# Attention scores of the first layer over three bfloat16 pieces in place of float32, with the exponentials one unit further behind

## The chip, the cores and the metric

The kernel runs on one core of a Trainium2 chip. The metric is the device time of the program in microseconds; the median of several runs counts. A core has five engines that run beside each other, each with its own queue of instructions in a fixed order: TensorE (PE in the profile, with its weight loads shown apart as PEld), VectorE (DVE), ScalarE (ACT), GpSimd (POOL) and SyncE (SP), which here only issues DMA transfers. They wait for each other by semaphores.

## The reference, cut to what matters

The program is a chain of residual blocks on a tensor of 4 batches x 512 tokens x 128 features, all float32:

```
x = x + 0.5 * latent_ffn(layernorm(x))   # causal attention, 16 heads of 8, then 8 experts, 2 chosen per token
x = x + attention(layernorm(x))          # full attention, 16 heads of 8
x = x + 0.5 * latent_ffn(layernorm(x))   # as the first
x = x + 0.5 * chosen_ffn(layernorm(x))   # attention of chosen tokens
x = x + additive_attention(layernorm(x)) # four layers
x = x + 0.5 * chosen_ffn(layernorm(x))
```

The change lies in the first three lines, which the kernel calls the first layer. What it computes there for every head (q and k have 8 values a token):

```
scores = q @ k.T / sqrt(8)          # causal: only keys up to the query
a      = exp(scores - max(scores)) / sum(exp(scores - max(scores)))
out    = a @ v
```

## The kernel before, in words

**Tasks and units.** The first layer is twelve tasks: four causal ones ("latent", one a batch), four full ones, four causal ones. A task's 16 heads lie as four groups g of four heads j. In the tiles `qA` and `kA` head j takes partitions 32j to 32j+31, so that a matmul of one head uses 32 of the array's 128 rows, and four heads can be multiplied at once on four strips of rows. A unit is one bank width of scores (512 columns) for all four heads of a group: 16 units in a full task. A causal task has 10, since the triangle is left out; four of them hold one piece of 512 columns, four hold 384 + 128, two hold 256 + 256.

**Two passes over the scores.** For each unit the queries are first multiplied with the keys (`maxima`, line 527) and VectorE takes the maximum of every row into `nms` (`reduce_max`: line 543 adds the causal mask and takes the maximum in one instruction, line 547 is the plain maximum of the full tasks). When a group is complete, `place_maxima` transposes its maxima (line 551) and four DMAs (line 555) write them into row 1 of each strip of `qA`; `kA` holds -1 in that row. Some units later `shifted` (line 562) multiplies again with keys and queries swapped, and this time the product comes out less the maximum. ScalarE takes its exponential (`exponent`, line 574), GpSimd zeroes the upper triangle of causal blocks (`mask`, line 580), and `products` (line 605) multiplies with the values.

**The order.** `attention` is one loop over units n. Every unit has two halves. In each half two heads of unit n go through `maxima` and two heads of an earlier unit through `shifted`, so four strips are busy; then come the maxima on VectorE, the exponentials, the mask, half of a unit's `products` two units later (`LAG`), and one piece of other work. `behind[n]` says which unit `shifted` takes: five units behind in the beginning (`FIRST`), one more from unit 26 (`HOLD`), at which `shifted` takes none. `GAP` is that distance; the next task but one may overwrite `qA` and `kA` (two sets, in turn) when it has passed.

**Other work beside it.** `prepare` makes a task's normalised input, queries `qC` and keys `kC` (lines 346 and 351, one ScalarE copy each out of PSUM). `spread` copies them by DMA to the strips of `qA` and `kA` (lines 359 and 360 for the first task, 363 to 366 for the others). `Mixture` computes the experts of a finished causal task (`hidden`: lines 467, 472, 473; `combined`), one step a half.

**What a scheduler decides.** The program is recorded by a layer that puts each engine's instructions in an order by its own estimate of when they are ready. That order is then fixed: an instruction that waits holds up all behind it on its engine. PSUM banks are chosen by `bank` with a small clock of its own.

Of the kernel before, what the change touches and what calls it, by code (L numbers as in the profile page):

```python
# [8 lines left out]
F32 = mybir.dt.float32  # L9
BF16 = mybir.dt.bfloat16  # L10
AF = mybir.ActivationFunctionType
ALU = mybir.AluOpType
AX = mybir.AxisListType

P = 128
B = 4
NC = 4
T = NC * P
NG = 4
NH = 16  # L20
HD = P // NH
FIRST, HOLD = 5, [26]
GAP, LAG = 6, 2
NE = 8
FH = 2
KSEL = T // 8
# [14 lines left out]
def tile_macaron(ctx: ExitStack, tc: tile.TileContext, a: dict, out: bass.AP):  # L41
    nc = tc.nc

    const = ctx.enter_context(tc.tile_pool(name="const", bufs=1))
# [6 lines left out]
    free, clock = [0.0] * 8, [0.0]  # L51
# [42 lines left out]
    causal = const.tile([P, T], F32, name="causal")  # L94
    paired = const.tile([P, P], BF16, name="paired")
    ones = const.tile([P, T], F32, name="ones")
    zeros = const.tile([4, T], F32, name="zeros")
    before = const.tile([P, NE, NE], F32, name="before")
    slots = const.tile([P, KSEL], F32, name="slots")
    places = const.tile([P, T], F32, name="places")  # L100
# [131 lines left out]
    def first_layer(opened, picked):  # L232
        with (
# [3 lines left out]
        ):  # L237
            hp = streaming.enter_context(tc.tile_pool(name="heads", bufs=1))

            qAs = [hp.tile([P, NG, T], F32, name=f"qA{i}") for i in range(2)]  # L240
            kAs = [hp.tile([P, NG, T], F32, name=f"kA{i}") for i in range(2)]
            vAs = [hp.tile([P, NC, NH, 32], F32, name=f"vA{i}") for i in range(2)]


            nc.vector.memset(qAs[0], 0.0)
            nc.vector.memset(kAs[0], -1.0)

            nms = [hp.tile([P, 32], F32, name=f"nm{g}") for g in range(NG)]
            for nm in nms:
                nc.gpsimd.memset(nm[:, 16:32], 0.0)  # L250

            def heads_constants():
                constants()
# [22 lines left out]
            class Task:  # L276
# [24 lines left out]
                def prepare(self):  # L301

                    b = self.b
# [7 lines left out]
                    v = small.tile([P, 2 * NC], F32, name="v2")  # L311
# [30 lines left out]
                    self.src = src  # L342
                    ps = bank()
                    by_columns(ps, wq, hT)
                    self.qC = wp.tile([P, T], F32, name="qC", bufs=1)
                    nc.scalar.activation(self.qC, ps, AF.Copy, scale=HD**-0.5)
                    yield
                    ps = bank()
                    by_columns(ps, wk, src)
                    self.kC = wp.tile([P, T], F32, name="kC", bufs=1)  # L350
                    nc.scalar.copy(self.kC, ps)
                    self.ready = True

                def spread(self):


                    if self.k == 0:
                        for g in range(NG):
                            nc.sync.dma_start(self.qA[0:P:4, g, :], self.qC[g:P:4, :])
                            nc.scalar.dma_start(self.kA[0:P:4, g, :], self.kC[g:P:4, :])  # L360
                        return
                    if self.k > 1:
                        nc.sync.dma_start(self.qA[1:P:32], zeros[0:4, :].unsqueeze(1).to_broadcast([4, NG, T]))

                    nc.sync.dma_start(self.qA[0:P:4], self.qC)
                    nc.sync.dma_start(self.kA[0:P:4], self.kC)

                def values(self):
                    pv = bank()
# [140 lines left out]
            def attention():  # L510
# [7 lines left out]
                def first(t, c, w):  # L518

                    return T - w, NC - 1 - c if t.causal else c  # L520

                def maxima(n, j):
                    t, unit = units[n]
                    ps = bank((2.0 if len(unit) == 1 else 2.3) + (0.8 if len(unit) == 1 else 1.1) * (j % 2))
                    r0 = 32 * j
                    for g, c, at, w in unit:
                        nc.tensor.matmul(  # L527
                            ps[:, at : at + w],
                            lhsT=t.qA[r0 : r0 + 32, g, c * P : (c + 1) * P],
                            rhs=t.kA[r0 : r0 + 32, g, 0:w],  # L530
                            start=True,
                            stop=True,
                        )
                    return ps

                def reduce_max(n, j, ps):
                    t, unit = units[n]
# [9 lines left out]
                            nc.vector.tensor_reduce(dst, src, axis=AX.X, op=ALU.max)  # L547

                def place_maxima(t, g):
                    mT = wp.tile([P, 32], F32, name="mT")  # L550
                    nc.vector.transpose(mT, nms[g])

                    to = t.qA[1:P:32, g, :].rearrange("j (c u q) -> j c u q", c=NC, u=4)
                    for u in range(4):
                        nc.sync.dma_start(to[:, :, u, :], mT[32 * u : 32 * u + 16, :])

                def shifted(n, j, ps):
                    t, unit = units[n]
                    r0 = 32 * j
                    for g, c, at, w in unit:  # L560
                        q0, kc = first(t, c, w)
                        nc.tensor.matmul(  # L562
                            ps[:, at : at + w],
                            lhsT=t.kA[r0 : r0 + 32, g, kc * P : (kc + 1) * P],
                            rhs=t.qA[r0 : r0 + 32, g, q0:T],
                            start=True,
                            stop=True,
                        )
                    return ps

                def exponent(n, j, ps):
                    if n not in es:
# [50 lines left out]

                behind = [None] * FIRST + list(range(HOLD[0] - FIRST))
                for h0, h1 in zip(HOLD, HOLD[1:] + [len(units) + GAP]):
                    x0 = behind[-1] + 1
                    behind += [None] + list(range(x0, x0 + h1 - h0 - 1))
                for n in range(len(units) + GAP + LAG):
                    now[0] = n
# [10 lines left out]
                    for part in range(2):  # L640
                        halves[0] += 1
                        sj, xj = (0, 1) if part == 0 else (2, 3), (2, 3) if part == 0 else (0, 1)
                        if n < FIRST:
                            sj = () if part else (0, 1, 2, 3)
                        xp, sp = [], []
                        if s is not None and n < 2 * FIRST:
                            sp = [maxima(s, j) for j in sj]
                        if x is not None:
                            xp = [shifted(x, j, bank(1.9 + 0.5 * i)) for i, j in enumerate(xj)]
                        if s is not None and n >= 2 * FIRST:  # L650
                            sp = [maxima(s, j) for j in sj]
                        clock[0] += 1.1
                        for j, ps in zip(sj, sp):
                            reduce_max(s, j, ps)
                        for j, ps in zip(xj, xp):
                            exponent(x, j, ps)
                        if x is not None and units[x][0].causal:
                            mask(x, xj[0])
                        one_hidden()
                        if y is not None:  # L660
                            products(y, part)
                        one_combined()
                        if part == 0:
                            for f in todo:
                                f()
                        step_background()
# [89 lines left out]
            nc.scalar.copy(f_wkv, ps[:, 0 : 2 * P])  # L756
            for _ in tasks[0].prepare():
                pass
            nc.vector.memset(qAs[1], 0.0)
            nc.vector.memset(kAs[1], -1.0)  # L760
            with tc.issue_after(last_root[0]):
                heads_constants()
            tasks[0].spread()
# [612 lines left out]
```

## Time and profile before

| what | value |
|---|---|
| median of 3 runs | 1371.02 us (1368.14 to 1375.04) |
| profiled execution: span from the first to the last instruction | 1369.7 us |
| profiled execution: time of its own outside the span | not recorded; the median is 1.3 us over the span |
| PE busy | 1289.1 us, 94% |
| DVE busy | 954.4 us, 70% |
| ACT busy | 586.5 us, 43% |
| POOL busy | 562.1 us, 41% |
| first `maxima` matmul starts | 17.36 us |
| last `maxima` of the twelfth task | 772.6 us |
| `maxima` matmuls of line 527 | 1536, 349.0 us busy |
| `shifted` matmuls of line 562 | 1536, 334.0 us busy |

How to read it: the page has two PE records for each float32 matmul of the program, so the 1536 of line 527 are 768 matmuls. Busy times of one engine overlap where matmuls run side by side. By the start of every 128th record of line 527 the tasks begin at 17.4, 57.1, 100.7, 167.2, 239.0, 347.6, 435.3, 496.1, 556.9, 599.8, 642.5 and 707.4 us. The experts' steps (line 473) run from 131.9 to 399.5 us and from 681.0 to 883.6 us. Everything after about 884 us is outside the change.

### The profile page before, as it was taken

The page shows a single profiled execution, that of the slowest core. Times are in us where ns is not written, and L with a number is a line of the kernel's source. Part 1 is how long each engine was busy: PE and PEld are TensorE (multiplying, and loading weights), DVE is VectorE, ACT ScalarE, POOL GpSimd, SP SyncE. Part 2 cuts the span into 40 slices and gives each one's busy share as a digit, 9 for nine tenths or more (in the row PEclk, how much of TensorE's full clock was granted, in tenths as well). Part 3 has the DMA queues.
Part 4 walks back from the last instruction along what each step waited for, and adds up shares of the span by engine and source line. Part 5 has one row for each costly group of instructions (what it writes and reads, how often), then busy time and mean ns, then how long its engine had stood idle before and what let it go on. Part 6 is the DMA issues. An engine that isn't in the chain of part 4 may idle for free. (4 is left out here: it accounts for less than half of the span.)

```text
span 1369.7 us, 29349 instructions
## 1 busy us (share of the span) xinstructions
PE 1289.1 (94%) x11050; PEld 699.9 (51%) x11050; DVE 954.4 (70%) x3293; ACT 586.5 (43%) x1180; POOL 562.1 (41%) x823
## 2 busy tenths in 40 slices
PE   5998999999999999999999999989889999997897
PEld 2554445333333333465544443367667767665675
DVE  6886776666658777778767638687466776667773
ACT  1555454454556666665545443222223332323222
POOL 8345655544424112024564755622244443543100
PEclk8999999999999999999999999999979999999799
DMA  3001101020111100000111011211000100000000
GB/s 115 21 24 41 43 33 49 2 80 1 64 45 32 39 1 18 3 19 19 50 33 34 33 53 28 76 40 40 1 20 5 40 1 17 1 1 1 1 9 23
DMA packets 37172, 39.52 MB, mean 29 GB/s; under 512 B 11080, under 2 KB 23880, under 8 KB 37032
## 3 DMA queue, kind: packets, MB, share of 16 engines
q1 hardware_dynamic: 34536, 35.06, 8.3%
q10 hardware_dynamic: 2496, 2.59, 0.6%
q8 instruction: 87, 1.43, 0.4%
q14 instruction: 53, 0.43, 0.1%
HBM read 29.45 MB, written 1.18 MB: 22 GB/s over the span
## 5 line engine op out<-in xcount | busy, mean ns | idle before, releaser
L574 ACT ACTIVATE e<-bank 128x512 f32<-128x512 f32 x576 | 313.7, 595 | 278.4 <-PE bank L527 240.0
L527 PE MATMUL bank<-kA,qA 32*128 32x512 f32 (+3 forms) x1536 | 349.0, 527 | 4.1 <-DVE nm L543 1.8
L562 PE MATMUL bank<-qA,kA 32*128 32x512 f32 (+3 forms) x1536 | 334.0, 524 | 0.3 <-DVE nm L543 0.3
L543 DVE CUSTOM_DVE_ANT_0 junk<-bank,causal 128x384 f32<-128x384 f32 (+3 forms) x512 | 251.0, 490 | 89.5 <-PE bank L527 51.3
L547 DVE TENSOR_REDUCE nm<-bank 128x1 f32<-128x512 f32 x256 | 164.9, 686 | 78.9 <-PE bank L527 78.7
L473 POOL TENSOR_TENSOR hid<-v,spread 128x512 f32<-128x512 f32 x128 | 163.9, 1286 | 127.1 <-DVE v L472 101.7
L562 PEld LDWEIGHTS bank<-qA,kA 32*128 32x128 f32 x1536 | 129.5, 185 | 136.9 <-issue 54.1
L605 PE MATMUL sum<-e,vA 128*32 128x256 f32 (+1 forms) x2560 | 183.7, 368 | 6.1 <-POOL e L580 6.0
L580 POOL TENSOR_SCALAR_AFFINE_SELECT e<-e 128x256 f32<-128x256 f32 x256 | 99.3, 407 | 192.8 <-ACT e L574 191.7
L527 PEld LDWEIGHTS bank<-kA,qA 32*128 32x128 f32 x1536 | 147.4, 187 | 24.6 <-DVE nm L543 5.8
L605 PEld LDWEIGHTS sum<-e,vA 128*32 128x32 f32 x2560 | 62.8, 109 | 165.8 <-issue 134.0
L267 PE MATMUL sum<-hid,sb_f_w 128*32 128x512 f32 x1024 | 135.6, 597 | 3.0 <-POOL hid L473 2.9
L267 PE MATMUL bank<-tT,sb_f_w 128*32 128x512 f32 x1024 | 137.1, 602 | 0.0
L472 DVE SCALAR_TENSOR_TENSOR v<-th,bank 128x512 f32<-128x512 f32 x128 | 87.0, 681 | 43.9 <-ACT th L467 29.2
L467 ACT ACTIVATE th<-bank 128x512 f32<-128x512 f32 x128 | 76.3, 597 | 49.0 <-PE bank L267 39.5
L154 POOL TENSOR_TENSOR r<-v,mhalf 128x4 f32<-128x4 f32 (+1 forms) x64 | 71.8, 1123 | 5.1
L1250 PE MATMUL bank<-h2T,w 128*128 128x512 f32 x128 | 69.0, 632 | 0.2 <-ACT h2T L1239 0.2
L1256 PE MATMUL bank<-w,hid 128*128 128x128 f32 x512 | 65.7, 277 | 0.1
L1256 PEld LDWEIGHTS bank<-w,hid 128*128 128x128 f32 x512 | 63.1, 194 | 4.8 <-issue 1.5
L1251 ACT ACTIVATE hid<-bank,sb_l_cols 128x512 f32<-128x512 f32 x64 | 43.9, 688 | 39.9 <-PE bank L1250 39.8
L1148 PE MATMUL bank<-wa,hT 128*128 128x385 f32 x128 | 56.5, 540 | 1.4 <-ACT hT L1141 1.4
L312 POOL TENSOR_SCALAR v<-mv 128x4 f32<-128x4 f32 x12 | 2.8, 230 | 131.1 <-DVE mv L171 130.8
(279 smaller groups left out, 1805.4 us busy)
## 6 DMA issues: line engine op xcount, KB each, us to landing
spread<-away SPq DMA_DIRECT2D x64, 256.0 KB
qA<-mT SPq DMA_DIRECT2D x192, 2.0 KB
qA<-qC SPq DMA_DIRECT2D x11, 256.0 KB
kA<-kC SPq DMA_DIRECT2D x11, 256.0 KB
w<-in_l_w_dram SPq DMA_DIRECT2D x8, 256.0 KB
sb_m_wqkv<-in_m_wqkv_dram SPq DMA_DIRECT2D x4, 384.0 KB
m_yg<-in_m_trig_dram SPq DMA_DIRECT2D x8, 130.0 KB
X<-in_x_dram SPq DMA_DIRECT2D x4, 256.0 KB
```

Source lines behind the costliest of these rows:

```text
L267: nc.tensor.matmul(ps[32 * j : 32 * j + 32, :], lhsT=w[:, 32 * j : 32 * j + 32], rhs=rhs, start=start, stop=stop, skip_group_check=True,)
L467: nc.scalar.activation(th, ph, AF.Tanh, scale=0.5)
L472: nc.vector.scalar_tensor_tensor(v, th, 1.0, ph, ALU.add, ALU.mult)
L473: nc.gpsimd.tensor_tensor(hid, v, self.spread[e], op=ALU.mult)
L527: nc.tensor.matmul(ps[:, at : at + w], lhsT=t.qA[r0 : r0 + 32, g, c * P : (c + 1) * P], rhs=t.kA[r0 : r0 + 32, g, 0:w], start=True, stop=True,
L543: nc.vector.tensor_tensor_reduce(junk[:, 0:w], src, causal[:, T - w : T], 1.0, NEG, ALU.add, ALU.max, dst)
L547: nc.vector.tensor_reduce(dst, src, axis=AX.X, op=ALU.max)
L562: nc.tensor.matmul(ps[:, at : at + w], lhsT=t.kA[r0 : r0 + 32, g, kc * P : (kc + 1) * P], rhs=t.qA[r0 : r0 + 32, g, q0:T], start=True, sto ...
L574: nc.scalar.activation(es[n][:, j, :], ps, AF.Exp)
L580: nc.gpsimd.affine_select(out=e, in_=e, pattern=[[0, 2], [1, P]], compare_op=ALU.is_ge, fill=0.0, base=0, channel_multiplier=-1,)
L605: nc.tensor.matmul(to[32 * j : 32 * j + 32, q0 + lo - at : q0 + hi - at], lhsT=t.vA[:, kc, 4 * j + g, :], rhs=es[n][:, j, lo:hi], start=fresh,
L1256: nc.tensor.matmul(pm[:, c * P : (c + 1) * P], lhsT=hid[:, f, c * P : (c + 1) * P], rhs=w2[:, f, :], start=(f == 0), stop=(f == 3),)
```

## The change

Queries, keys and maxima are each written as a sum of three bfloat16 numbers. The three pieces of a key lie in rows 0, 1, 2 of every four rows of the strip; three tiles `qA[0]`, `qA[1]`, `qA[2]` hold the three pieces of the queries, turned by one place from tile to tile, so that three bfloat16 matmuls that add up in one bank give all nine products. The negated row now takes four rows (3, 11, 19, 27) of a strip, three of which hold the pieces of the maximum.

In a half, the four strips now go round by round: first all matmuls with `qA[0]`, then all with `qA[1]`, then all with `qA[2]`. `pieces` replaces the single copy out of PSUM: ScalarE writes the first piece, VectorE the rest, GpSimd the second piece and the third. `place_maxima` splits the maxima by four GpSimd instructions ahead of the transposition, which becomes 128 columns wide. `spread` issues twelve DMAs of 128 KB where it issued two of 256 KB (eight of 64 KB for the first task). `behind` stands still at two units, 26 and 27, and `GAP` is 7.

```diff
-FIRST, HOLD = 5, [26]
-GAP, LAG = 6, 2
+FIRST, HOLD = 5, [26, 27]
+GAP, LAG = 7, 2
+NS = 3
...
-            qAs = [hp.tile([P, NG, T], F32, name=f"qA{i}") for i in range(2)]
-            kAs = [hp.tile([P, NG, T], F32, name=f"kA{i}") for i in range(2)]
+            qAs = [[hp.tile([P, NG, T], BF16, name=f"qA{i}{r}") for r in range(NS)] for i in range(2)]
+            kAs = [hp.tile([P, NG, T], BF16, name=f"kA{i}") for i in range(2)]
...
-            nc.vector.memset(qAs[0], 0.0)
-            nc.vector.memset(kAs[0], -1.0)
+            def fill(i):
+                for q in qAs[i]:
+                    nc.vector.memset(q.rearrange("p g t -> p (g t)").bitcast(F32), 0.0)
+                nc.vector.memset(kAs[i], -1.0)
+            fill(0)
...
-                    nc.scalar.activation(self.qC, ps, AF.Copy, scale=HD**-0.5)
+                    self.qC = self.pieces(ps, HD**-0.5, "q")
...
-                    nc.scalar.copy(self.kC, ps)
+                    self.kC = self.pieces(ps, 1.0, "k")
...
+                def pieces(self, ps, scale, name):
+                    x = [wp.tile([P, T], BF16, name=f"{name}C{s}", bufs=1) for s in range(NS)]
+                    rest = wp.tile([P, T], F32, tag="v", name="rest")
+                    nc.scalar.activation(x[0], ps, AF.Copy, scale=scale)
+                    nc.vector.scalar_tensor_tensor(rest, ps, scale, x[0], ALU.mult, ALU.subtract)
+                    nc.gpsimd.tensor_copy(x[1], rest)
+                    nc.gpsimd.tensor_tensor(x[2], rest, x[1], op=ALU.subtract)
+                    return x
...
-                    nc.sync.dma_start(self.qA[0:P:4], self.qC)
-                    nc.sync.dma_start(self.kA[0:P:4], self.kC)
+                    moves = [(self.kA[s:P:4], self.kC[s]) for s in range(NS)]
+                    moves += [(self.qA[r][s:P:4], self.qC[(s + r) % NS]) for r in range(NS) for s in range(NS)]
+                    for i, (to, x) in enumerate(moves):
+                        (nc.scalar if self.k == 0 and i % 2 else nc.sync).dma_start(to, x)
...
-                    for g, c, at, w in unit:
-                        nc.tensor.matmul(ps[:, at : at + w], lhsT=t.qA[r0 : r0 + 32, g, c * P : (c + 1) * P],
-                            rhs=t.kA[r0 : r0 + 32, g, 0:w], start=True, stop=True)
-                    return ps
+                    def product(r):
+                        for k, (g, c, at, w) in enumerate(unit):
+                            nc.tensor.matmul(ps[:, at : at + w], lhsT=t.qA[r][rows, g, c * P : (c + 1) * P],
+                                rhs=t.kA[rows, g, 0:w], start=r == 0 and k == 0, stop=r == NS - 1,
+                                skip_group_check=True)
+                    return ps, product
+
+                def in_rounds(*tiles):
+                    for r in range(NS):
+                        for _, product in tiles:
+                            product(r)
...
-                    mT = wp.tile([P, 32], F32, name="mT")
-                    nc.vector.transpose(mT, nms[g])
+                    m = nms[g].rearrange("p (j c) -> p j c", c=NC)
+                    split = pieces_of[g][:, :, 0:16].rearrange("p c (j s) -> p j s c", s=4)
+                    rest = wp.tile([P, 4, NC], F32, name="mR")
+                    nc.gpsimd.tensor_copy(split[:, :, 0], m)
+                    nc.gpsimd.tensor_tensor(rest, m, split[:, :, 0], op=ALU.subtract)
+                    nc.gpsimd.tensor_copy(split[:, :, 1], rest)
+                    nc.gpsimd.tensor_tensor(split[:, :, 2], rest, split[:, :, 1], op=ALU.subtract)
+                    mT = wp.tile([P, NC, 32], BF16, name="mT")
+                    nc.vector.transpose(mT, pieces_of[g])
...
-                        clock[0] += 1.1
+                        in_rounds(*xp, *sp)
+                        clock[0] += 0.7
```

`shifted` is changed in the same way as `maxima`, with the key pieces as weights and `qA[r]` streaming.

## The prediction

> **What bounds the kernel now.** First the page: its head, and the rows of the two score passes and the maxima.
>
> ```profile
> span 1369.7 us, 29349 instructions
> PE 1289.1 (94%) x11050; PEld 699.9 (51%) x11050; DVE 954.4 (70%) x3293; ACT 586.5 (43%) x1180; POOL 562.1 (41%) x823
> ...
> L527 PE MATMUL bank<-kA,qA 32*128 32x512 f32 (+3 forms) x1536 | 349.0, 527 | 4.1 <-DVE nm L543 1.8
> L562 PE MATMUL bank<-qA,kA 32*128 32x512 f32 (+3 forms) x1536 | 334.0, 524 | 0.3 <-DVE nm L543 0.3
> ```
>
> TensorE is the busy engine and waits little ahead of the scores. But the share is a mean over stages, so the view of busy time by stretch comes next, cut at the tasks' starts: a causal task without experts beside it, one with them, a full task with them, one without, and a causal one again.
>
> ```profile
> 57.10:100.70 43.60, 42.89 (x504) 23.47 (x500) 36.82 (x156) 26.14 (x49) 16.29 (x39) 1.00 0.08 23
> 167.20:239.00 71.80, 71.44 (x779) 33.71 (x775) 48.65 (x173) 36.46 (x68) 40.49 (x59) 1.00 0.12 40
> 239.00:347.60 108.60, 107.23 (x1002) 39.19 (x1001) 70.26 (x151) 53.86 (x101) 50.15 (x68) 0.97 0.08 26
> 435.30:496.10 60.80, 60.80 (x567) 21.36 (x563) 45.29 (x83) 38.66 (x73) 8.32 (x11) 1.00 0.10 31
> 556.90:599.80 42.90, 42.73 (x454) 23.59 (x450) 34.15 (x136) 25.65 (x49) 4.65 (x12) 1.00 0.05 15
> ```
>
> The columns are length, PE, PEld, DVE, ACT, POOL, clock, DMA. In the full tasks VectorE is idle for a quarter, so TensorE sets the pace. In the causal tasks without experts it does not: the view of waits gives VectorE only 1.0, 1.4, 3.8 and 3.0 us of waiting on TensorE between the first and last maximum of tasks 0, 1, 8 and 9 (tasks of 40 to 44 us); the rest of its "idle" is the 0.1 us between a maximum and the next. There **VectorE is the bound**.
>
> Last the timeline of one full half beside the experts, and the only bfloat16 matmul of the trace.
>
> ```profile
> 304.20 0.70 PE L562 MATMUL bank<-qA,kA 32*128 32x512 f32 x2
> 304.74 0.59 PE L562 MATMUL bank<-qA,kA 32*128 32x512 f32 x2
> 305.27 0.64 PE L267 MATMUL bank<-tT,sb_f_w 128*32 128x512 f32 x4
> ```
>
> ```profile
> L932 PEld LDWEIGHTS <-ident_h x32: 95/100/101, 909.3 to 1352.1; 128*128 128x128 bf16 x32
> L932 PE MATMUL bank<-paired,ident_h x32: 218/219/230, 909.4 to 1352.2; 128*128 128x128 bf16 x32
> ```
>
> A score half is two float32 passes on four strips at once, 304.20 to 305.27, 1.07 us: 0.11 for the first weight load, 2 x 0.43 of streaming, 0.11 until the next kind of tile begins.
>
> **The change, part by part.**
>
> *Rounds on TensorE.* A bfloat16 matmul of 128 columns takes 219 ns, a float32 one 277 (the row of L1256): 58 ns less for 128 columns, so a bfloat16 pass streams in half the time, 512 columns in 0.213. Three rounds are 0.64 against 0.853: **0.21 a half is saved**. Its weight load is 100 ns against the 187 of line 527, which could add 0.08 (upper end 0.30). Against that, a 128-column piece streams in only 53 ns and may not cover the next load, and no four-strip bfloat16 matmul is in the trace (lower end 0.10: half the gain lost). I take 0.22, the streaming and hardly more.
>
> The Trainium skill ("TensorE: Matmul & The Clock Gate", step 2 of Part 2) speaks against this: with hardware decode off, it says, about 62 ns of firmware go into each MATMUL. The densest 5 us of this trace (80.7 to 85.7) hold 81 matmul records, 62 ns each, without a stall, so it shows neither a faster issue nor that limit. By that rule a half of two-piece units, 24 score matmuls, would take 1.49 us of issue and gain nothing, and the sum below would be about 9 higher.
>
> Where it counts: some 72 halves with experts in causal tasks and after the last maxima (131.9 to 239.0 and 681 to 811): 72 x 0.22 = 15.8. Task 4: 32 x 0.22 = 7.0. The half of task 5 with experts: 3.5. The 80 full halves without experts are limited by VectorE next: it works 45.3 of 60.8 us (15.5 us of waiting in the view of waits), and gets 8.8 more (below), 54.1; TensorE's own is 60.8 - 7.0 = 53.8. With 0.5 for both waiting on each other, 54.6, 6.2 less a task, 15.5 for two and a half tasks. Together **-41.8**.
>
> *The start.* Nothing starts before all pieces of the first keys are in `kA`. The third comes from GpSimd, whose queue at that time is full. In the built program's order the first key's two instructions stand behind all constants and behind the next task's `r`, `h` and `Y`. The profile has those rows:
>
> ```profile
> 21.25 1.00 POOL L137 MEMSET mine<- 64x1 f32 x8
> 22.34 3.28 POOL L154 TENSOR_TENSOR r<-v,mhalf 128x8 f32<-128x8 f32 x2
> 25.62 3.13 POOL L323 TENSOR_SCALAR h<-X,mv,r 128x128 f32<-128x128 f32 x4
> 28.73 3.12 POOL L336 TENSOR_SCALAR Y<-X,mv,r 128x128 f32<-128x128 f32 x4
> ...
> 17.36 2.91 PE L527 MATMUL bank<-kA,qA 32*128 32x512 f32 x27 [0.90 <-DMA kA<-kC]
> ```
>
> The constants end at 20.07. Then, in the new order: query copy 0.7, eight memsets 1.1, two small ones 0.5, query subtraction 1.3, `r` 1.65, `h` 3.1, `Y` 3.1, two small 0.5, `r` 1.65, key copy 0.7, one `h` 0.8, key subtraction 1.3: 16.4, to 36.5. (Subtraction as line 473's 1.29. For the copy, between the 0.28 of a 128-column cast and 1.29, I take 0.7.) VectorE's memsets ahead (four, with 0.38 before each, for two) shift it by 0.8 to 1.6; with 1.2, 37.7. A key's DMA needs 1.97 from issue to the matmul (15.39 to 17.36), and two more DMAs of 0.63 stand behind it on SP before round three: 41.0. The first maximum is then ready for VectorE at 41.4 instead of 18.6. VectorE is the bound in this task, so all of it stays: **+23** (20.5 to 26).
>
> *VectorE in causal tasks without experts.* Each task gets two `rest` (line 472's 0.68): 1.4; four wider transpositions, 0.1 each by guess, 0.4; and four waits. The transposition stands in VectorE's order right after the group's last maximum, or one instruction later, and now waits for four dependent GpSimd instructions. The nearest row is such a chain:
>
> ```profile
> 158.02 0.56 POOL L679 TENSOR_TENSOR v<-mv 128x4 f32<-128x4 f32 x1 [0.93 <-DVE mv L171]
> 158.67 0.23 POOL L680 TENSOR_SCALAR v<-v 128x4 f32<-128x4 f32 x1
> 158.99 0.20 POOL L681 TENSOR_TENSOR v<-v,mv 128x4 f32<-128x4 f32 x1
> 159.27 1.04 POOL L154 TENSOR_TENSOR r<-v,mhalf 128x4 f32<-128x4 f32 x1
> ```
>
> Three take 1.25, a fourth 0.28, two handovers 0.1 each: 1.75 (0.9 if all are as the shortest, 3 if GpSimd is at something else). Queued behind it are the next maxima, and behind those TensorE, whose banks they hold. One maximum (0.52, 0.84, 0.52, none) stands between, so 5.1 a task; in full tasks none does, so 7.0. That is 6.9 a causal task and 8.8 a full one. Less the present waiting: 5.9, 5.5, 3.1, 3.9 in tasks 0, 1, 8 and 9: **+18.4**. The causal tasks beside experts have VectorE idle for a third, which covers it.
>
> *The rest.* `rest` also waits for ScalarE's first piece, queued behind exponentials: 0 to 6, I take 3. The second still unit at 27 leaves TensorE short of work there and pushes a unit to the end: 2 (0 to 3). `spread` puts twelve DMAs on SP, 7.6 us by 0.63 each; for the second task they stand ahead of the first task's later maxima: 0 to 7.6, I take 3. Later tasks issue theirs some three units (over 11 us) ahead of need, which covers them; a stall if units get shorter. ScalarE writes as much as before: 0.
>
> *Sum.* 23 + 18.4 + 3 + 2 + 3 - 41.8 = +7.6 on the span of 1369.7: 1377.3; with the 1.3 between span and median, which I leave, **1379**. The profiled execution lies inside the three timed ones.
>
> **Rivals.**
> - *TensorE's gain prevails* (0.29, faster). Weight loads vanish (0.30 a half) and GpSimd's chain takes 0.9, so that a transposition waits 0.5: gain 21.6 + 9.6 + 4.8 + 24 (51.2 us a full task) = 60, against 23 + 6 + 8: 1348; with only one of the two, 1364 to 1369. For it: the 100 ns load. Against it: VectorE's few microseconds of waiting in four tasks.
> - *Rounds gain nothing* (0.12, slower). Four strips at full rate disturb each other so that a round takes 0.32, not 0.21; three then take what the two float32 passes take. The 41.8 are gone: about 1421. Against it: float32 passes on four strips start within 0.02 us and run together; but at half the rate.
> - *SP's queue becomes the wait* (0.10, slower). Twelve moves ahead of the maxima's DMAs leave `shifted` waiting at each of tasks 2, 9 and 10 by some 3 us, as at the start: +9, 1388. It decides if a unit lasts under 2.5 us, since three units are the slack; now it lasts 4.
>
> **How the numbers follow.** My forecast, both effects nearly cancelling, has 0.49, in 1364 to 1394. Half a per cent, 7 us, is about what a measurement tells from no change; of the 0.49, 0.21 lie within it. So faster 0.29, same 0.21, slower 0.28 + 0.12 + 0.10 = 0.50. The low ends of all terms together give 1337, the high ends 1436; leaving out one in ten on either side, the range is 1347 to 1413.
>
> **What would show it.** Right: the first `maxima` matmul near 40 us; three rounds of about 0.22 in the timeline; full tasks without experts near 55 us, causal ones near 47; VectorE waiting for GpSimd at the transposition, 48 times. Wrong: a first matmul before 30 us, rounds of 0.3 or more, transpositions without a wait, or a late `qA<-mT` DMA ahead of `shifted`.

## The result, and the profile after

The changed kernel takes **1447.7 us** (1445.2 to 1449.0) against 1369.6 before: 1.056 times as long, 95% interval 1.0535 to 1.0592. The forecast was 1379. The profiled execution has a span of 1443.3 us, 73.6 over that of before.

First the page of the changed kernel: its head, the two score passes, and the transposition.

```profile
span 1443.3 us, 32811 instructions
PE 1254.3 (87%) x12586; PEld 652.5 (45%) x12586; DVE 969.4 (67%) x3321; ACT 585.2 (41%) x1180; POOL 651.5 (45%) x1063
...
L541 PE MATMUL bank<-kA,qA 32*128 32x512 bf16 (+3 forms) x2304 | 295.5, 348 | 76.2 <-DVE nm L564 35.4
L593 PE MATMUL bank<-qA,kA 32*128 32x512 bf16 (+3 forms) x2304 | 277.8, 342 | 31.7 <-DVE nm L568 17.5
L580 DVE STREAM_TRANSPOSE mT<-mp 128x128 bf16<-128x128 bf16 x48 | 15.0, 312 | 81.2 <-POOL mp L578 80.9
```

TensorE is busy 35 us less, and idle for 108 us ahead of the two score passes (22 of them at the start) where it was idle for 4. With 87% instead of 94% it is still the busiest engine, but now it waits itself, ahead of the scores. The last row says where that begins: VectorE's 48 transpositions stood 80.9 us for GpSimd.

The view of busy time by stretch, for the five tasks that the prediction showed (length, PE, PEld, DVE, ACT, POOL, clock, DMA):

```profile
86.10:135.10 49.00, 39.55 (x624) 17.71 (x623) 37.63 (x156) 25.27 (x47) 23.62 (x59) 0.95 0.15 44
213.20:289.70 76.50, 67.88 (x900) 28.21 (x900) 50.58 (x175) 35.39 (x67) 49.46 (x84) 0.93 0.18 52
289.70:391.20 101.50, 96.79 (x1169) 36.78 (x1169) 70.28 (x145) 54.20 (x103) 58.53 (x88) 0.98 0.12 39
482.50:547.00 64.50, 58.01 (x695) 19.77 (x692) 45.83 (x85) 38.76 (x73) 15.89 (x31) 0.95 0.16 47
612.10:660.90 48.80, 42.22 (x535) 17.02 (x533) 35.29 (x139) 25.08 (x46) 10.66 (x28) 0.86 0.13 36
```

They lasted 43.6, 71.8, 108.6, 60.8 and 42.9. Only the full task with experts became shorter. In the other four the clock was 1.00 before, and it is down in each.

A half beside the experts in the timeline: three rounds on four strips, 353 us in.

```profile
352.83 0.39 PE L593 MATMUL bank<-qA,kA 32*128 32x512 bf16 x2
352.84 0.39 PE L541 MATMUL bank<-kA,qA 32*128 32x512 bf16 x2
353.06 0.38 PE L593 MATMUL bank<-qA,kA 32*128 32x512 bf16 x2
...
353.27 0.38 PE L593 MATMUL bank<-qA,kA 32*128 32x512 bf16 x2
...
353.59 1.07 PE L274 MATMUL bank<-tT,sb_f_w 128*32 128x512 f32 x8
```

A round is 0.21 to 0.23 us, and the half ends after 0.76 where float32 took 1.07: 0.31 saved, more than the 0.22 of the forecast. So TensorE's gain came, and larger than forecast; the time went elsewhere. The next three fences are one moment of task 6: GpSimd's timeline, VectorE's, and TensorE's (the bracket is idle time and what ended it).

```profile
526.45 3.15 POOL L330 TENSOR_SCALAR h<-X,mv,r 128x128 f32<-128x128 f32 x4
529.59 3.13 POOL L343 TENSOR_SCALAR Y<-X,mv,r 128x128 f32<-128x128 f32 x4
532.66 0.25 POOL L575 CAST mp<-nm 128x16 bf16<-128x16 f32 x1
...
533.64 0.27 POOL L578 TENSOR_TENSOR mp<-mR,mp 128x16 bf16<-128x16 f32 x1
```

```profile
533.94 0.31 DVE L580 STREAM_TRANSPOSE mT<-mp 128x128 bf16<-128x128 bf16 x1 [5.98 <-POOL mp L578]
```

```profile
529.44 0.64 PE L638 MATMUL sum<-e,vA 128*32 128x256 f32 x8
534.88 0.61 PE L593 MATMUL bank<-qA,kA 32*128 32x512 bf16 x2 [4.80 <-DVE nm L568]
...
535.48 0.61 PE L593 MATMUL bank<-qA,kA 32*128 32x512 bf16 x2
```

The chain of four small instructions takes 1.25 us, as its rows before had promised, but it stands in GpSimd's order behind eight instructions of another task's layer norm (the rows of lines 330 and 343, 6.3 us). VectorE waits 5.98 us, no maximum is taken, no bank comes free, TensorE is dry for 4.80 us. Then it comes back slow. By stretch:

```profile
312.94:314.60 1.66, 0.01 (x1) 0.00 (x0) 1.49 (x6) 0.55 (x2) 0.77 (x2) 1.00 0.00 0
315.00:318.00 3.00, 3.00 (x27) 1.17 (x22) 1.89 (x6) 1.67 (x3) 1.32 (x5) 0.50 0.00 0
...
534.88:540.27 5.39, 5.39 (x42) 1.09 (x42) 3.88 (x7) 2.01 (x4) 0.00 (x0) 0.50 0.03 3
540.27:547.00 6.73, 6.50 (x87) 2.07 (x84) 4.91 (x9) 4.10 (x9) 0.00 (x0) 1.00 0.01 2
```

In the last two lines the granted clock is 0.50 for 5.4 us after the gap. So the gap cost more than its length: some 2.7 us more, half of the 5.4, by an estimate that takes TensorE to have had work all the while. The first two show a half clock behind a gap of only 1.66 us as well. Of the 48 transpositions five waited 5.9 to 10.1 us (37 us together); all others waited under 3. The expectations below speak of six such waits and 43 us; the trace has five.

The third place is the start, in GpSimd's order and TensorE's:

```profile
34.80 0.61 POOL L365 CAST kC<-rest 128x512 bf16<-128x512 f32 x1
35.40 0.81 POOL L330 TENSOR_SCALAR h<-X,mv,r 128x128 f32<-128x128 f32 x1
36.18 1.15 POOL L366 TENSOR_TENSOR kC<-rest,kC 128x512 bf16<-128x512 f32 x1
```

```profile
39.56 0.62 PE L541 MATMUL bank<-kA,qA 32*128 32x512 bf16 x4 [21.76 <-DMA kA<-kC]
```

The last piece of the first key is ready at 37.3 us, and the first score matmul comes at 39.6 instead of 17.4.

### The profile page after: what moved, and what is told of

It reads as the page before. It is cut to its first block, busy times and chain, and to the rows that moved or that the text cites. A ratio compares the mean times of both kernels' runs of the same rounds, so it can differ in the third digit from the quotient of the medians.

```text
span 1443.3 us, 32811 instructions
## 1 busy us (share of the span) xinstructions
PE 1254.3 (87%) x12586; PEld 652.5 (45%) x12586; DVE 969.4 (67%) x3321; ACT 585.2 (41%) x1180; POOL 651.5 (45%) x1063
## 5 line engine op out<-in xcount | busy, mean ns | idle before, releaser
L541 PE MATMUL bank<-kA,qA 32*128 32x512 bf16 (+3 forms) x2304 | 295.5, 348 | 76.2 <-DVE nm L564 35.4
L564 DVE CUSTOM_DVE_ANT_0 junk<-bank,causal 128x384 f32<-128x384 f32 (+3 forms) x512 | 250.1, 488 | 98.6 <-PE bank L541 58.6
L593 PE MATMUL bank<-qA,kA 32*128 32x512 bf16 (+3 forms) x2304 | 277.8, 342 | 31.7 <-DVE nm L568 17.5
L638 PE MATMUL sum<-e,vA 128*32 128x256 f32 (+1 forms) x2560 | 195.8, 391 | 9.3 <-POOL e L613 9.3
L593 PEld LDWEIGHTS <-kA 32*128 32x128 bf16 x2304 | 91.1, 95 | 224.3 <-issue 202.7
L541 PEld LDWEIGHTS <-qA 32*128 32x128 bf16 x2304 | 105.0, 96 | 95.7 <-issue 82.2
L274 PE MATMUL bank<-tT,sb_f_w 128*32 128x512 f32 x1024 | 140.0, 614 | 2.5 <-DVE v L484 2.3
L580 DVE STREAM_TRANSPOSE mT<-mp 128x128 bf16<-128x128 bf16 x48 | 15.0, 312 | 81.2 <-POOL mp L578 80.9
L1284 ACT ACTIVATE hid<-bank,sb_l_cols 128x512 f32<-128x512 f32 x64 | 44.0, 688 | 39.8 <-PE bank L1283 39.6
L575 POOL CAST mp<-nm 128x16 bf16<-128x16 f32 x48 | 12.3, 256 | 103.2 <-DVE nm L568 74.7
```

The source lines that it names most:

```text
L274: nc.tensor.matmul(ps[32 * j : 32 * j + 32, :], lhsT=w[:, 32 * j : 32 * j + 32], rhs=rhs, start=start, stop=stop, skip_group_check=True,)
L541: nc.tensor.matmul(ps[:, at : at + w], lhsT=t.qA[r][rows, g, c * P : (c + 1) * P], rhs=t.kA[rows, g, 0:w], start=r == 0 and k == 0, stop=r ...
L564: nc.vector.tensor_tensor_reduce(junk[:, 0:w], src, causal[:, T - w : T], 1.0, NEG, ALU.add, ALU.max, dst)
L593: nc.tensor.matmul(ps[:, at : at + w], lhsT=t.kA[rows, g, kc * P : (kc + 1) * P], rhs=t.qA[r][rows, g, q0:T], start=r == 0 and k == 0, sto ...
L638: nc.tensor.matmul(to[32 * j : 32 * j + 32, q0 + lo - at : q0 + hi - at], lhsT=t.vA[:, kc, 4 * j + g, :], rhs=es[n][:, j, lo:hi], start=fresh,
```

## The experiments

Two theories at first. **Q, the queue:** beyond the start, the time is lost by the transposition that waits behind GpSimd's other work, with the slow clock behind each gap. **R, the rounds:** the bfloat16 rounds themselves bring the clock down to 0.925. Medians are beside those of the kernel before on the same chip, 1368.5 to 1370.2.

**The chain on VectorE.**

```diff
-                    nc.gpsimd.tensor_copy(split[:, :, 0], m)
-                    nc.gpsimd.tensor_tensor(rest, m, split[:, :, 0], op=ALU.subtract)
...
+                    nc.vector.tensor_copy(split[:, :, 0], m)
+                    nc.vector.tensor_tensor(rest, m, split[:, :, 0], op=ALU.subtract)
```

> The changed kernel, with the four small instructions that split a group's maxima moved from GpSimd to VectorE; nothing is left out. Theory Q (the queue): the loss beyond the start comes from VectorE's transposition, which waits for four instructions that stand on GpSimd behind the next task's layer norm; six such waits are 5.9 to 10.1 us long (43 us together), TensorE runs dry and its granted clock falls after each. Then the long waits vanish (43), some 2.5 us of slow clock behind each go too (15), the 38 us of short waits turn into some 22 us of VectorE's own work (half of it on the path, 8 gained): about 1381 us (1370 to 1395), full tasks without experts near 53 us, mean clock about 0.95. Rival R (the rounds): TensorE's clock is 0.925 instead of 0.968 because of the bfloat16 rounds themselves. Then only the long waits' own time goes, 1400 to 1420, and the clock stays near 0.93.

Measured: 1403.4 us, ratio 1.0255 [1.0212, 1.0297], clock 0.941. The time lies in R's range, the clock between the two. The full tasks 6 and 7 took 58.6 and 58.9, not 53: the transpositions' waits for GpSimd were gone, and something else held these tasks.

**The first pieces on VectorE.**

```diff
-                    nc.gpsimd.tensor_copy(x[1], rest)
+                    eng = nc.vector if self.k == 0 else nc.gpsimd
+                    eng.tensor_copy(x[1], rest)
```

> The changed kernel, with the first task's second and third pieces of queries and keys computed on VectorE instead of GpSimd; nothing is left out. Both theories: the first score matmul moves from 39.6 to about 21 us and all of it shows in the time, since VectorE is the bound in that task: about 1429 us. If the start is covered by what follows, less than 10 us are gained.

Measured: 1432.9 us, 15 gained; the first score matmul at 25.1, not at the 21 expected.

**The wait alone, in float32.** Four dependent copies on GpSimd, ahead of the transposition of the kernel before:

```diff
-                    nc.vector.transpose(mT, nms[g])
+                    x = nms[g]
+                    for i in range(4):
+                        x, was = wp.tile([P, 32], F32, name=f"m{i}"), x
+                        nc.gpsimd.tensor_copy(x, was)
+                    nc.vector.transpose(mT, x)
```

> The kernel before, float32 scores and all, with four dependent GpSimd copies of the maxima put ahead of the transposition; nothing is left out. It has the changed kernel's waiting chain without its rounds. Theory Q: the transposition waits behind the same layer norms, TensorE runs dry six times and slows: plus 45 to 60 us, 1415 to 1430, mean clock about 0.93. Rival R: the clock stays at 0.968, float32 passes leave VectorE idle a quarter of the full tasks and hide a part: plus 10 to 30 us, 1380 to 1400.

Measured: 1434.7 us, ratio 1.0472 [1.0448, 1.0495], clock 0.955. From its waits (total, times, longest):

```profile
DVE mT L555 <- POOL m L554: 100.2, 48, 12.3
```

No bfloat16 score matmul is in this kernel, and it loses 66 us, twice R's most and more than Q's. R falls as the cause: such a wait alone is enough for a loss of this size, and takes the clock down with it, though not as far as Q had it. (Its waits are longer than the change's, 100.2 us against 80.9, so the 66 us are no measure of what the change's own waits cost.) A view further down says the same of R directly: full tasks with bfloat16 rounds run at a clock of 1.00.

**The lag alone.** The kernel before with the two still units and a distance of seven.

```diff
-FIRST, HOLD = 5, [26]
-GAP, LAG = 6, 2
+FIRST, HOLD = 5, [26, 27]
+GAP, LAG = 7, 2
```

> The kernel before, with exponentials seven units behind and a second still unit at 27, nothing else changed or left out. My term for it was 2 us (0 to 3): 1372. If the longer lag itself costs (an idle TensorE at the second still unit, a lower clock behind it), 1377 or more.

(One more line differs, and is that of the change: it counts the units for two still ones.) Measured: 1375.1 us, ratio 1.0038 [1.0021, 1.0055]: 3 to 8 us, over my 2.

**What held the full tasks.** A half of the chain-on-VectorE run, in TensorE's timeline and ScalarE's:

```profile
505.92 0.39 PE L593 MATMUL bank<-qA,kA 32*128 32x512 bf16 x2
505.96 0.86 PE L541 MATMUL bank<-kA,qA 32*128 32x512 bf16 x2
506.45 0.39 PE L593 MATMUL bank<-qA,kA 32*128 32x512 bf16 x2
...
506.68 0.38 PE L593 MATMUL bank<-qA,kA 32*128 32x512 bf16 x2
```

```profile
505.31 1.08 ACT L607 ACTIVATE e<-bank 128x512 f32<-128x512 f32 x2 [1.11 <-PE bank L541]
```

The first round begins at 505.92, the second only at 506.45. The two records of line 541 put together at 505.96 begin 0.49 us apart: the second maxima tile can begin its first round only when ScalarE's second exponential of the half before, ended at 506.40, has freed its bank (its wait in the trace is one on ScalarE). As all tiles go round by round, the other three stand behind it. The scores then need 0.61 us from there, the two exponentials 1.1 us, and the next half is tied to them again: halves of 1.8 us. In task 7 of this run 15 of 32 halves had scores longer than 1.2 us; unhindered they took 0.83. So theory **B**: the rounds are tied by their banks. The remedy changes only the costs by which banks are handed out:

```diff
-                    ps = bank((2.0 if len(unit) == 1 else 2.3) + (0.8 if len(unit) == 1 else 1.1) * (j % 2))
+                    ps = bank((1.6 if len(unit) == 1 else 1.9) + (0.6 if len(unit) == 1 else 0.9) * (j % 2))
...
-                            xp = [shifted(x, j, bank(1.9 + 0.5 * i)) for i, j in enumerate(xj)]
+                            xp = [shifted(x, j, bank(1.4 + 0.5 * i)) for i, j in enumerate(xj)]
...
-                        clock[0] += 0.7
+                        clock[0] += 0.8
```

> The kernel of the chain on VectorE, with other costs in the list that hands out the eight PSUM banks (1.4 and 1.9 us for exponentials, 1.6 and 2.2 for single maxima, 1.9 and 2.8 for double ones, 0.8 a half's scores): the second maxima tile of a half then takes the bank that the half before freed after its first exponential, not after its second. Nothing is left out. Theory B (the rounds are tied by their banks): since the four tiles' rounds are issued in turn, a late bank of the last tile holds the second and third rounds of the other three; the 1.8 us halves of the full tasks fall to about 1.4, 16 of 32 a task, full tasks from 58.7 to about 52.5, and the whole to 1375 to 1390 us. Rival: VectorE sets that pace, and nothing moves: 1400 to 1406.

Measured: 1384.2 us, ratio 1.0117 [1.0084, 1.0150]. Tasks 6 and 7 by stretch:

```profile
449.80:503.90 54.10, 52.98 (x692) 18.61 (x688) 48.82 (x100) 38.69 (x73) 11.88 (x15) 1.00 0.19 56
503.90:558.00 54.10, 52.97 (x692) 18.58 (x688) 48.82 (x100) 38.79 (x73) 11.89 (x15) 1.00 0.11 33
```

54.1 us a full task (58.6 before the remedy), and 4 of 32 long halves instead of 15. B holds.

**The transposition a unit later.** Chain on GpSimd as in the change, the transposition and its DMAs one unit on.

```diff
+                    later.append(lambda: place_pieces(t, g))
+
+                def place_pieces(t, g):
                     mT = wp.tile([P, NC, 32], BF16, name="mT")
                     nc.vector.transpose(mT, pieces_of[g])
```

> The changed kernel with its four small instructions on GpSimd where they are, and VectorE's transposition with its DMAs issued one unit later; nothing is left out. Theory Q: short waits (38 us in all) vanish and the six long ones lose one unit of 2.9 to 4 us each, VectorE gives up no time of its own: near the run with the chain on VectorE, 1395 to 1412 us, VectorE's wait for GpSimd under 25 us. Rival: the wait only moves, the exponentials' scores wait for the later DMA instead: 1430 or more.

Measured: 1446.2 us, nothing gained, and the waits of it are those of the change:

```profile
DVE mT L583 <- POOL mp L578: 79.4, 45, 9.8
```

In the timeline each transposition stood where it had stood: the ordering layer, by its own estimate, had moved it back behind its group's last maximum. The edit did not do what it said; that speaks neither for nor against Q.

**All three, with lag seven and with six.** That transposition with the bank costs and the early pieces; the last four lines stand in the lag-six run alone.

```diff
+                    eng = nc.vector if self.k == 0 else nc.gpsimd
...
+                def place_pieces(t, g):
...
-                        clock[0] += 0.7
+                        clock[0] += 0.8
...
-FIRST, HOLD = 5, [26, 27]
-GAP, LAG = 7, 2
+FIRST, HOLD = 5, [26]
+GAP, LAG = 6, 2
```

> All three together on the changed kernel: transposition a unit later, first pieces on VectorE, the other bank costs; nothing is left out. If the three losses are separate: 1447 less 40 (the wait), less 15 (the start, as measured), less 15 to 25 (the banks): 1367 to 1377, level with the kernel before. If they share the same time: 1385 or more.

> The same three edits, with exponentials six units behind and one still unit, as in the kernel before; nothing is left out. The lag of seven alone measured 5 us in the float32 kernel: if it costs the same here, 1360 to 1372 us; if the later transposition needs the seventh unit, the exponentials' scores wait for their DMAs and it is slower than the run with lag seven.

Measured: 1415.4 and 1425.1 us. The first lies far over the 1367 to 1377 expected. It is what start (15) and banks (19) give together, 1413.6, with nothing from the transposition, whose edit had no effect: those two losses are separate here. With lag six it is 10 us worse, as in the second of the two cases expected, but not for its reason: the exponentials' scores wait 1.3 us in all for the maxima's DMAs. The row that grew is the transposition's wait, 83.2 us with lag seven:

```profile
DVE mT L584 <- POOL mp L579: 104.1, 46, 12.5
```

Why GpSimd's chain comes later with lag six was not settled.

**The later place enforced**, by tying the transposition behind the last maximum issued so far:

```diff
+                    with tc.issue_after(last_max[0]):
+                        nc.vector.transpose(mT, pieces_of[g])
```

> As the run with the later transposition, but now the later place is enforced: each transposition is tied behind the last maximum issued by then, since without the tie the compiler's own ordering had put it back right behind its group's last maximum. Four to six maxima of the next group (3 to 5 us) now stand between. Nothing is left out. Theory Q: VectorE's wait for GpSimd falls from 81 to about 15 us, no other work is added to VectorE: 1385 to 1400 us, at or under the 1403 of the run with the chain on VectorE. Rival: the wait moves to the exponentials' scores behind the later DMA: 1425 or more.

Measured: 1422.4 us, ratio 1.0371 [1.0349, 1.0393], between the two ranges expected. Its waits:

```profile
DVE mT L584 <- POOL mp L578: 8.8, 4, 4.7
...
PE bank L597 <- DMA qA<-mT: 18.1, 11, 3.4
```

Q and its rival were both half right. VectorE's wait fell from 80.9 to 8.8 us, and the long gaps went; but a new wait came, 18.1 us of the exponentials' scores for the later DMA. Task 1, where the lag is still five, grew from 48.9 to 60.1 us, while tasks 8 and 9, where it is seven, fell from 48.8 and 48.3 to 41.8 and 45.4.

**With banks and start as well.** Two runs, one with the enforced transposition (the first lines below are its own), one with the chain on VectorE:

```diff
+                    with tc.issue_after(last_max[0]):
+                        nc.vector.transpose(mT, pieces_of[g])
...
+                    eng = nc.vector if self.k == 0 else nc.gpsimd
```

> The enforced later transposition with the first pieces on VectorE and the other bank costs; nothing is left out. If the three losses are separate: the run above less 15 (start) less 19 (banks): 1350 to 1366 us, faster than the kernel before. If they share time: 1370 or more.

> The chain on VectorE, the other bank costs, and the first pieces on VectorE; nothing is left out. 1384 less the 15 of the start: 1369 us (1364 to 1375), level with the kernel before. It lies above the run with the ordered transposition by VectorE's 0.95 us a group where VectorE sets the pace, some 4 us in each of four causal tasks.

Measured: 1392.3 and 1373.5 us (ratio of the second 1.0026 [1.0013, 1.0038]). The first missed for the reason just seen: against the second run its tasks 0 to 2 are 23.5 us longer, its tasks 8 to 11 13.1 us shorter. In the second the early pieces bring 10.7 us of the 15 that they brought alone.

**Put together.** The chain on VectorE up to task 7, on GpSimd with the enforced later place from task 8 on, the bank costs, and the first task's second piece on ScalarE; beside it the same with two rounds, which leaves out a third of the nine products, so that its scores are not the program's; and the change with the early pieces on ScalarE alone.

```diff
+                    if self.k == 0:
+                        nc.scalar.copy(x[1], rest)
+                        nc.vector.tensor_tensor(x[2], rest, x[1], ALU.subtract)
...
+                    eng = nc.gpsimd if t.k >= 8 else nc.vector
...
-                    for r in range(NS):
+                    for r in range(NS - 1):
```

The last two lines stand in the two-round kernel alone; the bank costs and the enforced place are those shown above.

> A version put together from the runs before: the other bank costs; the chain on VectorE in tasks 0 to 7 and on GpSimd with the tied later transposition from task 8 on (there the ordered run's tasks 8 to 11 were 4.1, 3.1, 3.8 and 2.1 us shorter than those of the VectorE run); the first task's second pieces cast on ScalarE, because VectorE's cast took 3.55 us beside GpSimd's memsets. Nothing is left out. 1373.5 less 13 less 4: 1356 us (1350 to 1364), faster than the kernel before by about 1%. If the gains of the late tasks are lost again in what follows them: 1366 to 1372.

> The mixed version with two rounds instead of three: a third of the nine products of both score passes is left out. It prices a round where the waits are gone. If TensorE is on the path in the stretches with experts and in the full tasks as I had it (112 halves and part of 80), some 0.21 us for each of 112 halves and 0.1 for 80: 30 us less, 1326. If VectorE, GpSimd's masks and the bank list set the pace by now, under 12 us less.

> The changed kernel with the first task's second piece cast on ScalarE and subtracted on VectorE, and nothing else; nothing is left out. With the casts on VectorE the first score matmul came at 25.1 us and 15 of the 22 us came back; without the 3.55 us cast beside the memsets it comes at 21 to 22 us, and the whole at 1428 to 1430. If the remaining loss is that of the twelve DMAs of the spread and not of the cast, 25 us again and 1433.

Measured: the mixed version takes **1355.3 us, ratio 0.9904 [0.9889, 0.9918]**, one per cent faster than the kernel before. Step by step: 1447.7 for the change, 1403.4 with the chain off GpSimd, 1384.2 with the bank costs, 1373.5 with the early pieces, 1355.3 with the late tasks' chain back on GpSimd and the first pieces on ScalarE. Its full tasks, and its task 8, by stretch:

```profile
433.90:488.00 54.10, 52.98 (x692) 18.62 (x688) 48.81 (x100) 38.69 (x74) 11.88 (x15) 1.00 0.19 56
542.20:583.40 41.20, 37.20 (x536) 15.34 (x535) 35.44 (x143) 24.98 (x46) 10.11 (x26) 1.00 0.15 43
```

With two rounds it takes 1331.8, 23.5 less, between the 30 and the 12 of the expectation. So TensorE is on the path again: the full tasks lose 3.5 to 4.6 us (task 5: 0.9), task 11 with the experts behind it 8.2, and tasks 8 and 9, which VectorE paces, nothing. The change with early pieces on ScalarE takes 1433.9, no better than on VectorE, though its first score matmul comes at 21.9. Its tasks 0 and 1 are 52.4 and 52.1 us long instead of 46.6 and 48.9: part of the early start is given back there. By which wait was not settled.

## Why the prediction was wrong, step by step

All runs against the profiled execution of before, in us, by the tasks' starts (task 11 up to its last `shifted` matmul):

| stretch | forecast | change | float32 with the chain | chain on VectorE | and banks | mixed |
|---|---|---|---|---|---|---|
| start of the first task | +23 | +22.2 | 0 | +22.1 | +22.1 | +4.5 |
| causal tasks without experts (0, 1, 8, 9) | +18.4 | +23.8 | +18.0 | +20.7 | +12.1 | +7.2 |
| causal tasks beside experts (2, 3, 10, 11) | -15.8 | +25.5 | +32.7 | +7.5 | +5.2 | +0.3 |
| full task 4 | -7.0 | -7.0 | -0.8 | -7.7 | -5.0 | -5.2 |
| full tasks 5 to 7 | -19.0 | +11.5 | +15.5 | -9.9 | -21.2 | -21.2 |

(The forecast had 8 more without a stretch of its own: the rests, the still unit and SP's queue. The change's rows add up to 76.0, against 73.6 between the spans; elsewhere it is 2.4 shorter. The span missed the forecast by 66 us: the third row missed by 41, the last by 31 and the second by 5; the 8, the 2.4 and a start that was 1 better go off that.)

*The start* was right: 39.6 us forecast as "near 40", 22.2 against 23.

*VectorE in causal tasks without experts* was right in kind and 5 us short (48.9, 48.8 and 48.3 us in tasks 1, 8 and 9 against "near 47", 46.6 in task 0). The float32 run gives +18.0 for its wait alone. With the chain on VectorE, where nothing waits, the row still has +20.7: there VectorE works some 3 us longer in each of these tasks instead.

*"The causal tasks beside experts have VectorE idle for a third, which covers it"* is the step that failed first. Idle time covers a wait only if the engine that lives on VectorE's results has work stored. It had little: the longest wait, 10.1 us in task 2, left TensorE dry for 7.4. The float32 run shows a price for this term, set at nothing, of +32.7 us; in the changed kernel, taking the chain off GpSimd brought 18.0 (from +25.5 to +7.5). Nor did the 15.8 us that the rounds were to gain here come when the wait was gone. In the mixed version TensorE is busy for 278 us in these four tasks, where it was 298 before, and the row stands at +0.3: TensorE is idle for the difference, in several waits, one of 8.3 us for GpSimd's mask among them. What holds these tasks was not settled.

*The wait itself*, 1.75 us, and 3 "if GpSimd is at something else", was mis-sized at its upper end. The mean of 45 waits is 1.80, almost the forecast, but by luck: forty are 1.1 in the mean, and five are 5.9 to 10.1. In four of the five "something else" was a layer norm of eight instructions, twice with its root as well; in the fifth (5.88 us, at 255 us) it was a mixture: a piece of a layer norm, an addition, masks and one of the experts' products. The layer norm's rows, 3.1 + 3.1 us, stood in the prediction itself, under the start, and was not used here. And a gap at TensorE was priced without the half clock behind it.

*The rounds* gained more than forecast: 0.31 a half against 0.22, the "upper end 0.30" at which the weight loads cost nothing more. That task 4 gives the -7.0 to the tenth is luck: 32 halves at 0.31 would be 9.9, and some 3 were lost again on the way. In the pure full halves "0.5 for both waiting on each other" was the mis-sized term: a late bank now stops all four tiles at once, since every later round stands behind the first round of the last tile. It took 4.5 us of each full task; with that and the wait gone, they take 54.1 against the forecast's 54.6. The closeness is TensorE's, busy for 53.0 (forecast 53.8); VectorE, forecast at 54.1 with its waits, is at 48.8 there.

*The lag* cost 5 (3 to 8) in the float32 kernel, not 2. In the changed kernel, with banks and start mended, lag seven was 10 us better than six, so this price does not carry over.

The rival "TensorE's gain prevails" had the rounds right (0.30), but not the waits, which it put at 0.5. The rival "rounds gain nothing" had the sign, but not the cause: rounds of 0.21, not 0.32. The rival of SP's queue did not decide; no wait on SP's DMAs beyond the start is among the large ones. Of the signs of the prediction, the first matmul, the rounds, the causal tasks and the waiting transpositions (45 of 48) came about as named; the full tasks near 55 us did not.

On the weighing against the Trainium skill: 24 score matmuls of two-piece units ran from 237.29 to 238.07 us, 0.78 us or 33 ns each. The rule of 62 ns of firmware a matmul ("TensorE: Matmul & The Clock Gate", Part 2, step 2), by which such a half would take 1.49 us of issue, set no limit here. The page ties it to hardware decode being off; no run here shows which decode was in use.

## What to carry to other kernels

An instruction that is moved to another engine costs what stands ahead of it in that engine's order, not only what it takes; list that order at the place where it will stand, and price the longest block in it. A wait in an engine that is idle a third of the time is not covered by that idleness if a third engine lives on what it frees, and a gap in TensorE can cost more than its length, by the slow clock behind it. When several tiles go round by round, the latest bank of any of them sets the pace of all: hand out banks by measured lives, or the gain of shorter rounds stays in the queue.

## What the runs showed of the hardware that was not expected

The granted clock falls even behind short gaps. After 4.80 us without a matmul it was 0.50 for 5.4 us; after 1.66 us (312.94 to 314.60) it was 0.50 from 315 to 318. In this trace the clock changes only on a grid of 3.41 us. By that grid, around the first gap and around the second:

```profile
530.01:533.42 3.41, 0.07 (x4) 0.09 (x1) 0.00 (x0) 0.49 (x2) 3.26 (x7) 1.00 0.00 0
533.42:536.83 3.41, 1.95 (x12) 0.38 (x11) 2.89 (x6) 0.22 (x1) 0.41 (x2) 0.50 0.03 3
536.83:540.25 3.42, 3.42 (x29) 0.70 (x28) 1.91 (x4) 1.77 (x4) 0.00 (x0) 0.50 0.03 2
311.56:314.97 3.41, 1.58 (x23) 0.49 (x18) 2.44 (x7) 1.68 (x4) 1.67 (x4) 1.00 0.01 2
314.97:318.38 3.41, 3.41 (x35) 1.44 (x28) 2.30 (x6) 1.67 (x3) 1.62 (x6) 0.50 0.00 0
```

The Trainium skill ("TensorE: Matmul & The Clock Gate", Part 1) has half rate behind an idle window of about 3.4 us, full rate behind a busy one, and free-running windows. The first gap agrees: TensorE was idle but for 0.07 us of the first line, the clock fell at its end, and it rose behind the third line, the first that was busy throughout. The second gap does not: TensorE was busy for 1.58 us of the fourth line, and the clock was 0.50 in the fifth all the same. So a gap of half a window's length can cost a whole window at half clock.

VectorE's cast of 512 columns, when GpSimd was clearing tiles, took 3.55 us, and the same cast of the key, later, 0.82. From the timelines of VectorE and GpSimd of the run with the chain on VectorE and early pieces:

```profile
15.70 3.55 DVE L366 CAST qC<-rest 128x512 bf16<-128x512 f32 x1
```

```profile
14.67 3.54 POOL L263 MEMSET vA<- 128x2048 f32 x2
18.16 1.34 POOL L266 MEMSET vA<- 128x256 f32 x4
```

The cast ends at 19.25 us, within the last memset (18.92 to 19.50), which took 0.58 us where the three before it took 0.30. In the mixed version ScalarE did the same cast beside the same memsets in 0.62. The Trainium skill ("SBUF — State Buffer", Who interferes with whom) says that a cast of VectorE's which uses both its ports and an instruction of GpSimd's exclude each other for the whole instruction, and that ScalarE has its own ports. The rows agree, and show more: the cast stood through five memsets in a row, not through one.
